# Turning depthwise kernels over on TensorE, wider Toeplitz loads, a deeper queue of rows, and an earlier place for the merging

## The chip, the core and the metric

The kernel runs on one core of one Trainium2 chip. The metric is the device time of one execution in microseconds (us), and the time before is the median of three runs. One more execution was taken by the hardware profiler; all rows below come from that one.

## The reference

The input `x` is float32, 8 images of 384 channels and 32 by 32 pixels. Four layers follow one another; everything is float32.

- Layer 0 is a two-directional state-space scan (16 states a channel over 1024 pixels) between dense projections, with a gated depthwise 3x3 convolution beside it.
- Layer 1 is a convolution block, a linear attention and a dense MLP with GELU.
- Layer 2 sums seven depthwise convolutions with their batch norms: one of 13x13 and six smaller, some dilated. All of them fit into 13x13, so the kernel merges them into one 13x13 kernel for each channel.
- Layer 3 is a 1x1 convolution with batch norm and a residual, then a depthwise 13x13 convolution with batch norm, to which a per-channel scale is added, and GELU:

```python
x_pw = bn(einsum('bchw,oc->bohw', x, pw_w), ...) + x
out = bn(dwconv(x_pw, dwk_w), ...)
out = out + bn(x_pw * dw1_w, ...)
return gelu(out, approximate=False)
```

## The kernel before, in words

**The layers 0 and 1** (`_layers01`). For each image b the function `front(b)` makes the inputs of the scan, `scan(b)` scans, and `layer1(b)` (called `seconds[b]`) does the rest. `scan(b)` has 48 units of work (`rounds = 48`), each with two steps. A step makes `da` on ScalarE (line 840), `du` on VectorE (line 845), two scans on VectorE (line 857), and one product on GpSimd (line 866); TensorE then sums over the states (lines 546, 551). Between the units a hand-written planner calls the generators in `jobs`, each given as [generator, total cost, first unit, last unit, done]: whichever is furthest behind its due share is advanced, until none is behind. During scan b, `front(b+1)` and `seconds[b-1]` are advanced. During the first scan there is also `fold()`, which folds norms into weights and fills `x2_d` with zeros. A scheduler of the framework then orders each engine's instructions; they run in that order.

**Merging the depthwise kernels** (`kernels`, called `prepare`). For each of three groups of 128 channels and for each of the two 13x13 convolutions, GpSimd clears a tile `g` (line 199 or 215), VectorE adds the scaled kernels into it with channels on partitions (`merge`, lines 184 and 186), and a DMA on GpSimd's queue writes `g` to DRAM (line 210 into `g2_d`, line 224 into `g3_d`). In DRAM the layout is [channel, 4 shifts, 63 rows, 4 taps]. The planner is told to do this with cost 7 during the second scan (units 48 to 96).

**The depthwise convolutions** (`conv`). A convolution in the direction of rows is a product with a Toeplitz matrix: for one channel, one shift e and one tap t, the 32 by 32 matrix is read out of the 63 rows by letting row j begin one row later than row j-1. `load_windows` reads such overlapping windows for a block of 8 channels: four DMAs, one for each shift, each of 32 partitions times 8 channels times 128 floats. The tile `tp` is [128, 8 channels, 32 rows x 4 taps], and there are 20 of them. The first 20 blocks are loaded by `windows` from GpSimd's queue behind the last scan, the others from the queues of SyncE and ScalarE up to ten blocks ahead (line 245).

The pixels of a block come as `xt` [128, 8, 313]: one DMA on GpSimd's queue (line 296) fills 32 partitions with the padded rows, and two VectorE copies (`shift`, line 302) make the three shifted images on the other 96. There are four such tiles and `conv` loads two blocks ahead. A block has 64 products of a 128x32 weight with 256 columns (line 326), in two PSUM tiles. The weight is

```python
tp[:, c, :].rearrange("p (j t) -> p j t", t=KT)[:, :, t]
```

so its 32 columns lie 4 floats apart.

The first convolution (tag "a", 48 blocks) evicts to `yt` on VectorE and ScalarE by turns and writes `y2_d` with one DMA for two blocks (line 344). Then the 1x1 convolution runs, 16 steps from `y2_d` to `xp_d` (lines 365 to 388). The second convolution (tag "b") reads `xp_d`; ScalarE applies GELU from PSUM into `ot` (line 394, six tiles), and GpSimd's queue writes the result, one DMA for four channels (line 395). On GpSimd's queue each `xt_b` load therefore stands between the outputs of earlier blocks, in program order.

Of the kernel before, what the change touches and what calls it, by code (L numbers as in the profile page):

```python
# [10 lines left out]
FP = mybir.dt.float32  # L11
# [29 lines left out]
N_WIN, NCH = 20, 8  # L41
N_REP, N_DA, N_HS = 6, 4, 8
AHEAD = 5000
TP = H * KT
PADW = KS // 2
HIMG = H // 2 * (W + 2)
UL = L + 6
# [21 lines left out]
def tile_layers(  # L69
# [40 lines left out]
    x2_d = dram.tile([C, H, RL], FP, tag="x2_d", name="x2_d")  # L110
    y2_d = dram.tile([C, H, B, W], FP, tag="y2_d", name="y2_d")
    xp_d = dram.tile([C, H, RL], FP, tag="xp_d", name="xp_d")
    g2_d = dram.tile([C, NSH, TG, KT], FP, tag="g2_d", name="g2_d")
    g3_d = dram.tile([C, NSH, TG, KT], FP, tag="g3_d", name="g3_d")
# [47 lines left out]

    bias2 = const.tile([P, NC, 1], FP, tag="bias2", name="bias2")

    def kernels(small, large):

        off = H - 1 - KS // 2

        def merge(g, src, k, d, scale, first):
            lo = KS // 2 - d * (k // 2)

            step = NSH // gcd(NSH, d)
            for a in range(min(step, k)):
                n = len(range(a, k, step))
                kx = lo + d * a
                dst = g[
                    :, kx % NSH, off + lo : off + lo + d * (k - 1) + 1 : d,
                    kx // NSH : kx // NSH + (n - 1) * (d * step // NSH) + 1 : d * step // NSH,  # L180
                ].rearrange("p b a -> p a b")
                sv = src[:, a::step, :]
                if first:
                    nc.vector.tensor_scalar_mul(dst, sv, scale)
                else:
                    nc.vector.scalar_tensor_tensor(dst, sv, scale, dst, ALU.mult, ALU.add)

        def column(t, n, name):
            return t[:, :n].rearrange("p (q i t) -> p q i t", q=NSH, i=TG)

        bias3 = const.tile([P, NC, 1], FP, tag="bias3", name="bias3")
        dlt = const.tile([P, NC, 1], FP, tag="dlt", name="dlt")
        gn = NSH * TG * KT
        for c in range(NC):
            kw = small(f"kw_{c}")
            ktot = sum(k * k for k, _ in _L2K)
            nc.sync.dma_start(kw[:, :ktot], l2k[c * P : (c + 1) * P, :])
            t = large(f"g2_{c}")
            nc.gpsimd.memset(t[:, :gn], 0.0)
            g = column(t, gn, "g2")  # L200
            at = 0
            for j, (k, d) in enumerate(_L2K):
                src = kw[:, at : at + k * k].rearrange("p (a b) -> p a b", b=k)
                at += k * k
                merge(g, src, k, d, bns(f"l2_{j}", c), j == 0)
# [18 lines left out]
            nc.gpsimd.dma_start(g3_d[c * P : (c + 1) * P].rearrange("p q i t -> p (q i t)"), t[:, :gn])  # L224
            yield 1
# [8 lines left out]
    def load_windows(g_d, tag, n, queues):  # L234

        if not wins:
            wins["pool"] = ctx.enter_context(tc.tile_pool(name="win", bufs=1, side="right"))
        tp = wins["pool"].tile([P, NCH, TP], FP, tag="tp", name=f"tp_{tag}_{n}", bufs=N_WIN)
        for e in range(NSH):
            at = H * ((n % 2 * 2 + e) % NSH)  # L240
            win = bass.AP(
                g_d.tensor, g_d[NCH * n, e, 0, 0].offset,
                [[KT, H], [NSH * TG * KT, NCH], [1, TP]],
            )
            queues[e % len(queues)].dma_start(tp[at : at + H], win)
        wins[tag, n] = tp

    def windows(queues):
# [8 lines left out]

    NQ = C // 4
    GB = 4
    with tc.tile_pool(name="cw", bufs=1, reuse_waits="tile") as cwp, tc.tile_pool(  # L260
        name="cx", bufs=2, reuse_waits="tile"
    ) as cxp, tc.tile_pool(
        name="cps", bufs=6, space=PSUM, reuse_waits="tile"
    ) as cps:
        xos = []
        for i in range(3):
            t = cwp.tile([P, NC, 2, RL], FP, tag=f"xo{i}", name=f"xo{i}")
# [4 lines left out]
        gbias = cwp.tile([P, NQ], FP, tag="gbias", name="gbias")  # L272
        for q in range(4):
            nc.scalar.dma_start(gbias[q * H : (q + 1) * H, :], biasq_d[q, :].partition_broadcast(H))
        def conv(g_d, src_d, tag, put):

# [8 lines left out]
            def load(n):  # L285
                for m in range(n, min(n + 1 + N_WIN // 2, NB_C)):
                    if (tag, m) not in wins:
                        load_windows(g_d, tag, m, [nc.sync, nc.scalar])
                if n >= NB_C:
                    return  # L290
                at = places(n)
                xt = cxp.tile([P, NCH, RL], FP, tag="xt", name=f"xt_{tag}_{n}", bufs=4)
                src = bass.AP(
                    src_d.tensor, src_d[NCH * n, 0, 0].offset, [[RL, H], [H * RL, NCH], [1, RL]],
                )
                nc.gpsimd.dma_start(xt[at[0] : at[0] + H], src)  # L296
                xts[n] = xt
# [7 lines left out]
                    )  # L305


            for n in range(2):
                load(n)
            shift(0)  # L310
            for g in range(NQ):
                n, first = divmod(4 * g, NCH)
                if first == 0:
                    load(n + 2)
                    if n + 1 < NB_C:
                        shift(n + 1)
                    xt, tp = xts.pop(n), wins[tag, n]
                ps = cps.tile([P, HALF], FP, tag="cv", name=f"cv_{tag}_{g}")
                for t in range(KT):
                    for e in range(4):  # L320
# [5 lines left out]
                        nc.tensor.matmul(  # L326
                            ps[H * e : H * (e + 1), 0:BW],
                            tp[:, c, :].rearrange("p (j t) -> p j t", t=KT)[:, :, t], rhs,
                            start=(t == 0), stop=(t == KT - 1), skip_group_check=True,
                        )  # L330
                put(g, ps[:, 0:BW])
# [3 lines left out]

        def put2(g, ps):
            if g % GB == 0:
                hold["t"] = cxp.tile([P, GB, BW], FP, tag="yt", name=f"yt_{g}")
            if g % 2:
                nc.scalar.copy(hold["t"][:, g % GB, :], ps)  # L340
            else:
# [21 lines left out]
        xf = xp_d.rearrange("(k p) h r -> p k h r", p=P)  # L363
        NB = 2 * BW
        for t in range(H // 2):
            yt = cxp.tile([P, NC, NB], FP, tag="yp", name=f"yp_{t}", bufs=3)
            nc.sync.dma_start(yt, yf[:, :, t * NB : (t + 1) * NB])
            xo = xos[t % 3]
            for m in range(NC):
                ps = cps.tile([P, HALF], FP, tag="cv", name=f"pw_{t}_{m}")  # L370
                for k in range(NC):
# [4 lines left out]
                tm = cxp.tile([P, NB], FP, tag="tm", name=f"tm_{t}_{m}", bufs=3)  # L376
# [19 lines left out]
                ov[g * P : (g + 1) * P], ot.rearrange("p (b w) -> p b w", w=W)  # L396
            )

        conv(g3_d, xp_d, "b", put3)


def _layers01(tc, nc, B, xv, x2_d, dram, ident, mean_w, eps5, eps6, one, half, minus1, vec, bns, bnt,
# [12 lines left out]
    with ExitStack() as ctx:  # L415
# [78 lines left out]
        def psum(name):  # L494
            return psp.tile([P, HALF], FP, tag="mm", name=name, bufs=2)
# [430 lines left out]
                nc.gpsimd.dma_start(dst.rearrange("(k p) o -> p k o", p=P), w)  # L926
                yield 5

        prepare = kernels(t2, lambda name: sp.tile([P, NC * C], FP, tag="w", name=name, bufs=N_W))

        def phi(dst, ps, name):

# [380 lines left out]
```

## Time and profile before

| what | us |
|---|---|
| median of three runs (5093.32 to 5104.8) | 5100.76 |
| the profiled execution, and its span | 5049.81, 5048.0 |
| first scan, from its first product on GpSimd to that of the second scan | 530.2 |
| second scan | 500.4 |
| third and fourth scan | 493.9 and 492.9 |
| last scan, with no `front` beside it | 426.0 |
| the rest of the last image's layer 1 | 366.6 |
| first depthwise convolution | 211.8 |
| 1x1 convolution, to the first product of the next | 150.1 |
| second depthwise convolution, to the end | 252.9 |

The stages follow one another, and the rows come from the view of windows with the starts of the first instructions as bounds. Busy shares over the whole span (PE 83%, DVE 75%, POOL 59%, ACT 52%) are averages over stages with different limits, so each stage is read by itself. In what follows PE is TensorE, PEld its weight loads, DVE is VectorE, ACT ScalarE, POOL GpSimd and SP SyncE.

### The profile page before, as it was taken

What the parts mean: (1) busy time and instruction counts of PE and PEld (TensorE: products, weight loads), DVE (VectorE), ACT (ScalarE), POOL (GpSimd) and SP (SyncE); (2) the same over time, 40 slices, a digit from 0 to 9 for tenths busy, and PEclk for the clock granted to TensorE, in tenths of its full rate; (3) what the DMA queues carried; (4) which work ended last, traced back from release to release, by engine and by line L of the source; (5) the groups of instructions that cost most, each with busy time, mean ns of one, the idle gap of its engine ahead of it and who ended that gap; (6) DMA issues with size and microseconds to landing.
All of it is one profiled execution on the core that took longest, in us unless ns stands there. A gap on an engine that the chain in (4) does not pass through costs nothing. (4 is left out here: it accounts for less than half of the span.)

```text
span 5048.0 us, 58439 instructions
## 1 busy us (share of the span) xinstructions
PE 4205.7 (83%) x20128; PEld 1787.7 (35%) x20128; DVE 3789.3 (75%) x3861; ACT 2632.2 (52%) x3735; POOL 2975.1 (59%) x1546
## 2 busy tenths in 40 slices
PE   7555568898989998988888898988888869978877
PEld 2211113332333333333333333333333324466366
DVE  1689889988988898788978887888898821066256
ACT  3546435784577557756765676568546613100211
POOL 1467567676666676666666666666776750032156
PEclk9676779899989998999899999999898979999989
DMA  8975556577657765776567646765754581399686
GB/s 229 276 235 180 178 157 208 204 219 195 216 181 217 202 215 176 215 207 217 180 199 214 223 170 195 231 211 174 181 169 133 160 177 41 71 215 233 212 189 142
DMA packets 543121, 965.28 MB, mean 191 GB/s; under 512 B 56569, under 2 KB 220905, under 8 KB 542825
## 3 DMA queue, kind: packets, MB, share of 16 engines
q1 hardware_dynamic: 401648, 663.89, 44.2%
q0 software_dynamic: 58048, 205.76, 15.4%
q10 hardware_dynamic: 83128, 91.90, 6.4%
q8 instruction: 159, 2.61, 0.2%
q14 instruction: 138, 1.12, 0.1%
HBM read 726.36 MB, written 234.98 MB: 190 GB/s over the span
## 5 line engine op out<-in xcount | busy, mean ns | idle before, releaser
L866 POOL TENSOR_TENSOR hs<-hs,bct 128x1024 f32<-128x1024 f32 x768 | 2418.2, 3149 | 939.6 <-DVE carry L862 422.9
L840 ACT ACTIVATE da<-dlt,neg_a 128x512 f32<-128x512 f32 x1536 | 1036.7, 715 | 1055.1 <-DVE hs L857 987.9
L857 DVE TENSOR_TENSOR_SCAN hs<-da,carry,du 128x512 f32<-128x512 f32 x768 | 942.7, 1266 | 175.3 <-PE acc L551 129.8
L845 DVE TENSOR_TENSOR du<-vr,bct 128x1024 f32<-128x1024 f32 x768 | 1019.2, 1327 | 46.3 <-DMA vr<-v_d 34.9
L857 DVE TENSOR_TENSOR_SCAN hs<-da,du 128x512 f32<-128x512 f32 x768 | 900.8, 1208 | 128.6 <-PE acc L551 59.9
L551 PE MATMUL acc<-hs,selt 128*32 128x512 f32 x2304 | 546.7, 663 | 140.9 <-POOL hs L866 140.7
L533 PE MATMUL mf<-ln,w 128*128 128x512 f32 x1152 | 546.1, 620 | 22.8 <-DMA w<-w_d 11.7
L1166 PE MATMUL mo<-hm,w 128*128 128x512 f32 x1152 | 530.3, 599 | 13.8 <-DVE xx L1133 13.8
L546 PE MATMUL acc<-hs,selt 128*32 128x512 f32 x768 | 428.5, 653 | 74.4 <-POOL hs L866 63.7
L533 PEld LDWEIGHTS mf<-ln,w 128*128 128x128 f32 x1152 | 222.0, 200 | 331.7 <-issue 270.4
L533 PE MATMUL in<-xn,win 128*128 128x512 f32 x576 | 295.7, 654 | 44.0 <-DMA win<-in_inproj_t 23.6
L1166 PEld LDWEIGHTS mo<-hm,w 128*128 128x128 f32 x1152 | 214.7, 190 | 307.5 <-issue 281.2
L840 ACT ACT_TABLE_LOAD x233 | 298.9, 1283 | 9.5 <-DMA dw_i<-h_d 3.0
L326 PE MATMUL cv_b<-xt_b,tp_b 128*32 128x256 f32 x3072 | 193.6, 407 | 67.9 <-DVE xt_b L302 44.1
L302 DVE COPY xt_b<-xt_b 32x2496 f32<-32x2496 f32 x96 | 147.8, 1540 | 108.0 <-DMA xt_b<-xp_d 103.9
L326 PE MATMUL cv_a<-xt_a,tp_a 128*32 128x256 f32 x3072 | 186.0, 390 | 47.6 <-DVE xt_a L302 21.4
L1136 POOL DMA_DIRECT2D x_d<-xx x48 | 56.5, 1179 | 281.4 <-DVE xx L1133 274.1
L551 PE MATMUL dw<-dw_i,t3b 96*32 96x512 f32 x1056 | 205.6, 656 | 11.1 <-DMA dw_i<-h_d 11.0
L533 PE MATMUL op<-g,wo 128*128 128x512 f32 x288 | 156.4, 695 | 61.3 <-DMA g<-g_d 61.3
L326 PEld LDWEIGHTS cv_b<-xt_b,tp_b 128*32 128x32 f32 x3072 | 163.8, 141 | 98.0 <-issue 69.3
L533 PEld LDWEIGHTS in<-xn,win 128*128 128x128 f32 x576 | 114.1, 207 | 215.2 <-issue 161.5
L326 PEld LDWEIGHTS cv_a<-xt_a,tp_a 128*32 128x32 f32 x3072 | 159.7, 138 | 74.3 <-issue 28.7
(196 smaller groups left out, 5724.7 us busy)
## 6 DMA issues: line engine op xcount, KB each, us to landing
dlt<-dl_d SPq DMA_DIRECT2D x384, 256.0 KB, 4.6
vr<-v_d SPq DMA_DIRECT2D x384, 256.0 KB, 5.0
bct<-bc_d SPq DMA_DIRECT2D x256, 256.0 KB, 3.7
ut<-u_d SPq DMA_DIRECT2D x192, 257.5 KB, 5.5
lc_i<-xn_d SPq DMA_DIRECT2D x192, 228.8 KB, 5.4
dw_i<-h_d SPq DMA_DIRECT2D x192, 228.8 KB, 5.6
w<-w_d SPq DMA_DIRECT2D x64, 576.0 KB, 6.1
w<-in_w SPq DMA_DIRECT2D x64, 576.0 KB, 5.9
```

The source lines that it names most:

```text
L302: nc.vector.tensor_copy(xt[at[e] : at[e] + e * H, :, 0 : RL - e - (e - 1)], xt[at[0] : at[0] + e * H, :, e : RL - (e - 1)],)
L326: nc.tensor.matmul(ps[H * e : H * (e + 1), 0:BW], tp[:, c, :].rearrange("p (j t) -> p j t", t=KT)[:, :, t], rhs, start=(t == 0), stop=(t = ...
L533: product = nc.tensor.matmul(ps, w[:, k, m * P : (m + 1) * P], rhs[k] if isinstance(rhs, list) else rhs[:, k, :], start=(k == 0), stop=(k ...
L546: first = product()
L551: tc.keep_in_program_order(product())
L840: nc.scalar.activation(da[:, bass.ts(j, HALF)], dlt[:, bass.ts(j, HALF)], AF.Exp, scale=neg_a[:, g, r : r + 1],)
L845: nc.vector.tensor_mul(pairs(du), pairs(vt), bct[r][:, 0:1, :].to_broadcast([P, 2, HALF]),)
L857: nc.vector.tensor_tensor_scan(t[:, s][:, way], da[:, s][:, way], du[:, s][:, way], k_c if second else 0.0, ALU.mult, ALU.add,)
L866: made.append(nc.gpsimd.tensor_mul(pairs(t), pairs(t), bct[r][:, 1:2, :].to_broadcast([P, 2, HALF])))
L1136: nc.gpsimd.dma_start(x2v[m, :, h * (H // 2) : (h + 1) * (H // 2), PADW + b * (W + PADW) : PADW + b * (W + PADW) + W,], rows(o),)
L1166: nc.tensor.matmul(acc[m], wb[:, f, m * P : (m + 1) * P], hm, start=(i == 0 and f == 0), stop=(i == FF // C - 1 and f == NC - 1),)
```

## The change

- `kernels` gets a PSUM allocator. After a kernel tile `g` is merged, `put_columns` turns it over: for each of the four shifts, four products with the identity put [63 rows, 128 channels] for each tap into PSUM, VectorE copies them into a tile in the order channel, tap, and a DMA on GpSimd's queue writes that tile to DRAM. `g2_d` and `g3_d` become [48 blocks, 4 shifts, 63 rows, 8 channels x 4 taps].
- `load_windows` reads, for each of the 32 partitions, one contiguous piece of 32 rows x 8 channels x 4 taps (4096 bytes); `tp` becomes [128, 32 rows, 8 channels, 4 taps], and the weight is `tp[:, :, c, t]`, whose columns lie 32 floats apart.
- `conv` takes the distance of its loads as `far`: 2 for the first convolution and 5 for the second. The second has three more tiles for rows, `xu`, in the place of the pool `cw`, which is closed after the 1x1 convolution; the tiles `yt`, `yp` and `tm` move into that pool.
- The planner is told to merge with cost 31 during the first scan (units 0 to 48).

```diff
-    g2_d = dram.tile([C, NSH, TG, KT], FP, tag="g2_d", name="g2_d")
+    g2_d = dram.tile([C // NCH, NSH, TG, NCH * KT], FP, tag="g2_d", name="g2_d")
...
+        def put_columns(g_d, g, c, name):
+            for q in range(NSH):
+                ps = psum(f"{name}_{c}_{q}")
+                for t in range(KT):
+                    nc.tensor.matmul(
+                        ps[:TG, t * P : (t + 1) * P], g[:, q, :, t], ident, start=True, stop=True,
+                        skip_group_check=True,
+                    )
+                o = small(f"{name}t_{c}_{q}")
+                nc.vector.tensor_copy(
+                    o[:TG, :].rearrange("i (c t) -> i t c", t=KT), ps[:TG, :].rearrange("i (t c) -> i t c", t=KT)
+                )
+                nb = P // NCH
+                nc.gpsimd.dma_start(
+                    g_d[c * nb : (c + 1) * nb, q].rearrange("n i e -> i n e"),
+                    o[:TG, :].rearrange("i (n e) -> i n e", n=nb),
+                )
...
-            nc.gpsimd.dma_start(g2_d[c * P : (c + 1) * P].rearrange("p q i t -> p (q i t)"), t[:, :gn])
-            yield 1
+            put_columns(g2_d, g, c, "p2")
+            yield 5
...
-        tp = wins["pool"].tile([P, NCH, TP], FP, tag="tp", name=f"tp_{tag}_{n}", bufs=N_WIN)
+        tp = wins["pool"].tile([P, H, NCH, KT], FP, tag="tp", name=f"tp_{tag}_{n}", bufs=N_WIN)
...
             win = bass.AP(
-                g_d.tensor, g_d[NCH * n, e, 0, 0].offset,
-                [[KT, H], [NSH * TG * KT, NCH], [1, TP]],
+                g_d.tensor, g_d[n, e, 0, 0].offset, [[NCH * KT, H], [1, H * NCH * KT]],
             )
...
-                xt = cxp.tile([P, NCH, RL], FP, tag="xt", name=f"xt_{tag}_{n}", bufs=4)
+                if "pool" in more and n % 7 >= 4:
+                    xt = more["pool"].tile([P, NCH, RL], FP, tag="xu", name=f"xt_{tag}_{n}")
+                else:
+                    xt = cxp.tile([P, NCH, RL], FP, tag="xt", name=f"xt_{tag}_{n}", bufs=4)
...
-                    load(n + 2)
+                    load(n + far)
...
-                            tp[:, c, :].rearrange("p (j t) -> p j t", t=KT)[:, :, t], rhs,
+                            tp[:, :, c, t], rhs,
...
-        conv(g2_d, x2_d, "a", put2)
+        conv(g2_d, x2_d, "a", put2, 2)
...
-        conv(g3_d, xp_d, "b", put3)
+        mid_ctx.close()
+        with tc.tile_pool(name="xu", bufs=3, reuse_waits="tile") as more["pool"]:
+            conv(g3_d, xp_d, "b", put3, 5)
...
-        jobs = [[fold(), 36, 0, rounds, 0], [prepare, 7, rounds, 2 * rounds, 0]]
+        jobs = [[fold(), 36, 0, rounds, 0], [prepare, 31, 0, rounds, 0]]
```

More of the change, by code (lines that the diff above doesn't have):

```diff
@@ L43 @@
 AHEAD = 5000
-TP = H * KT
 PADW = KS // 2
@@ L112, in tile_layers @@
     xp_d = dram.tile([C, H, RL], FP, tag="xp_d", name="xp_d")
-    g2_d = dram.tile([C, NSH, TG, KT], FP, tag="g2_d", name="g2_d")
-    g3_d = dram.tile([C, NSH, TG, KT], FP, tag="g3_d", name="g3_d")
+    g2_d = dram.tile([C // NCH, NSH, TG, NCH * KT], FP, tag="g2_d", name="g2_d")
+    g3_d = dram.tile([C // NCH, NSH, TG, NCH * KT], FP, tag="g3_d", name="g3_d")
     bias_d = dram.tile([C], FP, tag="bias_d", name="bias_d")
@@ L163, in tile_layers, with kernels @@
     bias2 = const.tile([P, NC, 1], FP, tag="bias2", name="bias2")
-    def kernels(small, large):
+    def kernels(small, large, psum):
         off = H - 1 - KS // 2
@@ L223, in kernels @@
             nc.vector.tensor_add(bias3[:, c, :], bnt("dwk", c), bnt("dw1", c))
-            nc.gpsimd.dma_start(g3_d[c * P : (c + 1) * P].rearrange("p q i t -> p (q i t)"), t[:, :gn])
-            yield 1
+            put_columns(g3_d, g, c, "p3")
+            yield 5
         with nc.allow_non_contiguous_dma(reason="384 biases"):
@@ L241, in load_windows @@
             win = bass.AP(
-                g_d.tensor, g_d[NCH * n, e, 0, 0].offset,
-                [[KT, H], [NSH * TG * KT, NCH], [1, TP]],
-            )
-            queues[e % len(queues)].dma_start(tp[at : at + H], win)
+                g_d.tensor, g_d[n, e, 0, 0].offset, [[NCH * KT, H], [1, H * NCH * KT]],
+            )
+            queues[e % len(queues)].dma_start(
+                tp[at : at + H].rearrange("p j c t -> p (j c t)"), win
+            )
         wins[tag, n] = tp
@@ L259, in tile_layers @@
     GB = 4
-    with tc.tile_pool(name="cw", bufs=1, reuse_waits="tile") as cwp, tc.tile_pool(
-        name="cx", bufs=2, reuse_waits="tile"
-    ) as cxp, tc.tile_pool(
+    with tc.tile_pool(name="cx", bufs=2, reuse_waits="tile") as cxp, tc.tile_pool(
         name="cps", bufs=6, space=PSUM, reuse_waits="tile"
     ) as cps:
+        gbias = cxp.tile([P, NQ], FP, tag="gbias", name="gbias", bufs=1)
+        mid_ctx = ExitStack()
+        cwp = mid_ctx.enter_context(tc.tile_pool(name="cw", bufs=1, reuse_waits="tile"))
+        more = {}
         xos = []
@@ L271, in tile_layers, with conv @@
         nc.scalar.dma_start(pwt, pw_t.rearrange("(k p) o -> p k o", p=P))
-        gbias = cwp.tile([P, NQ], FP, tag="gbias", name="gbias")
         for q in range(4):
             nc.scalar.dma_start(gbias[q * H : (q + 1) * H, :], biasq_d[q, :].partition_broadcast(H))
-        def conv(g_d, src_d, tag, put):
+        def conv(g_d, src_d, tag, put, far):
             xts = {}
@@ L305, in shift @@
                     )
-            for n in range(2):
+            for n in range(far):
                 load(n)
@@ L337, in put2 @@
             if g % GB == 0:
-                hold["t"] = cxp.tile([P, GB, BW], FP, tag="yt", name=f"yt_{g}")
+                hold["t"] = cwp.tile([P, GB, BW], FP, tag="yt", name=f"yt_{g}", bufs=2)
             if g % 2:
@@ L365, in tile_layers @@
         for t in range(H // 2):
-            yt = cxp.tile([P, NC, NB], FP, tag="yp", name=f"yp_{t}", bufs=3)
+            yt = cwp.tile([P, NC, NB], FP, tag="yp", name=f"yp_{t}", bufs=3)
             nc.sync.dma_start(yt, yf[:, :, t * NB : (t + 1) * NB])
@@ L375, in tile_layers @@
                     )
-                tm = cxp.tile([P, NB], FP, tag="tm", name=f"tm_{t}_{m}", bufs=3)
+                tm = cwp.tile([P, NB], FP, tag="tm", name=f"tm_{t}_{m}", bufs=3)
                 nc.scalar.activation(
@@ L927, in fold @@
                 yield 5
-        prepare = kernels(t2, lambda name: sp.tile([P, NC * C], FP, tag="w", name=name, bufs=N_W))
+        prepare = kernels(t2, lambda name: sp.tile([P, NC * C], FP, tag="w", name=name, bufs=N_W), psum)
         def phi(dst, ps, name):
```

## The prediction

> **What bounds the kernel now.** I read the busy shares by stage first (view of windows: length, busy us of PE, PEld, DVE, ACT, POOL, granted clock, DMA share, GB/s). The rows below are scan one, two and three, the first depthwise convolution ("a") and the second ("b").
>
> ```profile
> 145.60:675.80 530.20, 296.50 (x1048) 92.74 (x1048) 458.31 (x433) 263.80 (x372) 330.87 (x164) 0.68 0.63 202
> 675.80:1176.20 500.40, 434.14 (x1668) 164.88 (x1669) 435.81 (x480) 320.66 (x444) 341.18 (x160) 0.92 0.67 202
> 1176.20:1670.10 493.90, 442.21 (x1698) 169.66 (x1697) 425.03 (x423) 323.59 (x448) 332.68 (x148) 0.94 0.67 203
> ...
> 4433.20:4645.00 211.80, 185.52 (x3070) 159.70 (x3072) 155.69 (x142) 17.51 (x47) 65.89 (x68) 0.98 1.08 244
> ...
> 4795.10:5048.00 252.90, 193.55 (x3072) 163.74 (x3072) 144.85 (x94) 45.49 (x96) 154.84 (x140) 0.94 0.79 165
> ```
>
> Both convolutions do the same 3072 products, but b takes 41 us more; in b no engine and no DMA is full. In scan one PE is light (297 of 530) and DVE is the fullest (458). Next the page's costliest groups, for who is waited for in b:
>
> ```profile
> L326 PE MATMUL cv_b<-xt_b,tp_b 128*32 128x256 f32 x3072 | 193.6, 407 | 67.9 <-DVE xt_b L302 44.1
> L302 DVE COPY xt_b<-xt_b 32x2496 f32<-32x2496 f32 x96 | 147.8, 1540 | 108.0 <-DMA xt_b<-xp_d 103.9
> ```
>
> PE waits for the shift, and the shift for the landing of the rows. The timelines of PE, DVE and POOL show why:
>
> ```profile
> 4846.75 4.93 PE L326 MATMUL cv_b<-xt_b,tp_b 128*32 128x256 f32 x82
> 4856.28 6.02 PE L326 MATMUL cv_b<-xt_b,tp_b 128*32 128x256 f32 x74 [4.61 <-DVE xt_b L302]
> ```
>
> ```profile
> 4852.91 3.27 DVE L302 COPY xt_b<-xt_b 32x2496 f32<-32x2496 f32 x2 [5.99 <-DMA xt_b<-xp_d]
> ```
>
> ```profile
> 4847.39 0.59 POOL L296 DMA_DIRECT2D xt_b<-xp_d  x1
> 4847.98 1.86 POOL L395 DMA_DIRECT2D out<-ot  x2
> 4849.83 0.59 POOL L296 DMA_DIRECT2D xt_b<-xp_d  x1
> 4850.75 0.89 POOL L395 DMA_DIRECT2D out<-ot  x1 [0.33 <-ACT ot L394]
> 4852.56 0.89 POOL L395 DMA_DIRECT2D out<-ot  x1 [0.92 <-ACT ot L394]
> 4853.43 1.42 POOL L296 DMA_DIRECT2D xt_b<-xp_d  x1
> 4860.42 0.92 POOL L395 DMA_DIRECT2D out<-ot  x1 [5.57 <-ACT ot L394]
> ```
>
> It is a ring. A load is issued only after outputs that wait for ACT, which waits for PE; the load issued at 4847.39 landed at 4852.8, its two copies ended at 4856.2, and PE, which had run dry 4.6 us before, began. With loads two blocks ahead the ring (issue, 5.6 us median to landing, two copies of 1.45) is longer than two blocks of PE work. After the stop PE also runs at half pace for about 4 us: four products start every 0.43 us there, every 0.215 us elsewhere. Blocks come in threes of about 8.5, 5.2 and 3.5 us, and the shortest, 3.48, is PE's own pace (16 x 0.2155).
>
> **Second convolution, far = 5.** The ring is cut: seven tiles, loads five blocks ahead, at least 17 us for a chain of about 9. What is late next? For a block: PE 3.48. DVE two copies, 2.9. POOL one load and two outputs. Alone these cost 0.593 and 0.888, 2.37 in all; but of the 48 loads the 27 that overlap a DVE copy have a mean of 1.32, and of the 96 outputs the 59 that do have 1.30. DVE will copy for some 75% of the time, so I take the overlapped row: 1.32 + 2 x 1.30 = 3.9 us, and POOL becomes the bound by a little. DMA: the stage moved 165 GB/s x 252.9 us = 41.7 MB; in 193 us that is 216 GB/s, and a moves 244 with smaller pieces. So 48 x 3.9 plus the 5.7 from the last product to the end = 193, **-60**. Bounds: PE's pace 3.48 gives 173 (-80); a's present pace, 211.8/48 = 4.41, gives 217 (-35).
>
> The Trainium skill (SBUF — State Buffer, sections "SBUF: two separate sides" and "A bandwidth-pool intuition that's wrong") speaks against this: a DMA issued from GpSimd's queue cannot write its descriptors while a float32 SBUF copy on VectorE holds their shared port, and it gives some 3.1 us for such an issue instead of 0.62. By that figure three issues would cost 9.3 us a block, and the stage would be 452 us by my estimate from it. The row for it here is the 1.30 to 1.32 us above, at most 2.16; the measured rows decide.
>
> **Windows in one piece.** In the first convolution 48,225 of the 58,268 DMA packets are 512 bytes, 44 ns each, 61% of the engines' time; the packets of 4096 bytes there take 47 ns a KB against 88. DMA is at 1.08, so landings (8.0 us for `xt_a`) should get shorter. But a is not bound there: the order of DVE's queue is the same in the changed program, and in it a shift stands behind an eviction that waits for PE. The repeating four blocks take 17.5 us, of which one wait for a landing is 0.68. Twelve times 0.68 is 8; I take **-4**, bounds -12 and 0. The 80 window DMAs on POOL behind the last scan (0.58 each) have nobody waiting behind them; 0, or -5 if the 15.5 us for which PE waits on `g_d` there shrink.
>
> The weights' columns now lie 128 bytes apart instead of 16. The trace has no such load. Contiguous 128x32 loads take 114 ns (`acc`), those 16 bytes apart 138 and 141. From below the cost is 0; from above I take the same step once more, 28 ns. Products start every 54 ns with four loads overlapping, so 28 ns would be 6144 x 28 / 4 = 43 us. I take 0: the step already separates all columns, and it is nearest to the row of 16 bytes.
> The Trainium skill (SBUF — State Buffer, section "Door 1: The DMA port swizzle", on 16-byte lines) says that each access crossing into a new line of 16 bytes pays a penalty; by it both layouts pay alike, and the cost is 0. No run here shows that.
>
> **Scans one and two.** The merging has 75 DVE operations, 36.9 us (12 forms summed in the groups of 600 to 1060 us). But the scheduler already begins them at 618: only 7.75 + 6.38 = 14.1 us lie in the second scan, and 22.8 at the end of the first. So the first scan gets 14 us of DVE more, and 24 new copies from PSUM: the nearest row, `zr<-acc` 128x512 out of PSUM, is 0.68, so 16.5 us (10 at the 256-column row, 33 if the reordering doubles it). DVE has 530.2 - 458.3 = 72 us idle there, mostly in the first 120 us, where the fill of `x2_d` has DMA at 0.8 to 0.98; the first of the six groups falls there. I put half of the 31 on the path: +15.
> POOL issues 24 DMAs instead of 6: nearest rows are 1.18 (`x_d<-xx`, 128x16x32 pieces) and 0.76 (`xn_d<-zero`), so 18 to 28 us, less 6 x 0.55. They stand between the products of line 866 and wait for the DVE copy, which waits for PE: while such a DMA waits, the next scan products wait on POOL, then PE's sums. POOL is 331 of 530 busy and can catch up; I take one us for each group of four, +6.
> PE gets 96 products 63x128; at the 0.28 us of a 128x128 weight load these are 27 us in a stage with 230 idle: 0. Without that cover, 27.
> The second scan loses its merging and should be like its followers: 500.4 to 493.4, -7.
> Sum for the scans **+14**, from -7 (all in idle time) to about +50.
>
> **Total.** -60 - 4 + 14 = -50. The profiled execution, 5049.8, would be 5000. The three runs had a median of 5100.8, 1.0% above it; by the same microseconds that gives 5050. A change of less than 0.2%, 10 us, can't be told from none (the three runs themselves spread over 11.5).
>
> **Rivals.**
> - *The first scan pays for everything.* The ring DVE to POOL to PE there is tight, and every hand-over of `put_columns` (two PSUM tiles, shared with `front`) stalls it: 31 of DVE, 25 of POOL and 24 hand-overs of 2 us, 104 - 7 = +97. Total +33: 5134. It decides from the point where the first scan is longer than 530 + 64 + 7 = 601 us. For it: DVE 86% busy, merges of up to 2.3 us where a POOL product was running. Against: the 14 us in scan two cost only 7. Chance 0.14.
> - *Only the wait changes its name in b.* POOL stays in order, with outputs that wait for ACT, so that the pace is that of the last sixteen blocks now, 4.68: 48 x 4.68 + 5.7 = 230, -22. Total -12: 5089. Against it: those blocks still waited for landings. Chance 0.14.
> - *The weight loads slow PE*, both convolutions by 43 us (-7 in total, 5094), or by 172 if nothing overlaps (5223). From 50 us / 6144 = 8 ns a product it is no gain. Chance 0.06.
> - *All of it hidden*, b at 3.48: -80 - 8 - 7 = -95, 5006. Chance 0.10.
> - The forecast, 5050, its own range 5015 to 5085: 0.56.
>
> **Range and chances.** 5008 to 5100 leaves out the first rival, most of the third, and half of the last. Faster: 0.55 of the forecast, 0.08 of the second rival, 0.01 and 0.10, 0.74. Slower: 0.14 + 0.04 + 0.01 = 0.19. The rest, 0.07, is no difference.
>
> **What would show it.** Right: b near 193 us with few waits of the shifts on `xp_d`, POOL over 85% busy in it, issue times of 1.3; a at 205 to 211 with packets of 4 KB; scan one 545 to 560, scan two about 493; PEld of `cv_a` still near 138 ns. Wrong: b still over 225, scan one over 600, or products of b starting more than 60 ns apart inside a block.

## The result and the profile after

The changed kernel takes 5057.56 us (median of four runs, 5055.1 to 5066.84), beside 5102.78 us for the kernel before in the same session (5093.32 to 5114.69). The ratio is 0.9914, with a 95% interval of 0.9889 to 0.9938: it is faster, by 45 us. Run a second time, as e4 below, it gave 0.9900 [0.9884, 0.9917], 51 us. The forecast was 5050, 50 us faster.

The profiled execution took 5066.84 us, its span 5065.1. The profile of the kernel before came from an execution 1% shorter than the median of its runs (5049.81 against 5100.76), so differences of stages are taken from a second profile of the kernel before, e0 (span 5143.5, scans three to six 503 to 506 us as in the changed kernel, where they are 502 to 509). Stages by the bounds of the table of before, in us; only a and the 1x1 convolution part at the first product of the 1x1 here, some 11 us later than there:

| stage | before, e0 | after | after again, e4 | e4 - e0 |
|---|---|---|---|---|
| first scan | 532.4 | 562.4 | 566.3 | +34 |
| second scan | 506.2 | 490.2 | 492.0 | -14 |
| scans three to eight | 2945.7 | 2934.7 | 2948.9 | +3 |
| rest of the last image's layer 1 | 377.8 | 360.0 | 362.7 | -15 |
| a, from its first product to the first of the 1x1 | 229.7 | 222.5 | 222.3 | -7 |
| 1x1 convolution | 140.5 | 139.1 | 139.9 | -1 |
| b, to the end | 258.0 | 203.9 | 205.0 | -53 |
| start | 153.1 | 152.4 | 151.3 | -2 |

The last column adds up to -55, the difference of the two spans (5143.5 - 5088.5); the medians give 51. e0 and e4 come from two sessions (medians of before 5129.92 and 5140.79), and the profiled execution of e0 was the slowest of its eight (5145.33, median 5133.21), so a difference of a few us may be the spread of the profiles. Against the first profile of before, the rest of layer 1 (366.6 there, 360.0 after) gains 7 us, and a (222.8 to the first product of the 1x1, 222.5 after) nothing. It is the forecast's picture, with other sizes: b gives the gain, the first scan gives some back, and a stage to which the forecast gave nothing gives up to 15 us more.

The view of windows of the changed kernel, with the columns as before (length, busy us of PE, PEld, DVE, ACT, POOL, granted clock of PE as a share of full speed, mean busy share of the DMA engines, GB/s). The rows are scan one, two and three, a to its last product, and b:

```profile
152.40:714.80 562.40, 329.21 (x1267) 122.96 (x1264) 488.97 (x517) 267.59 (x375) 360.81 (x191) 0.71 0.67 201
714.80:1205.00 490.20, 427.52 (x1641) 159.44 (x1640) 425.84 (x420) 313.74 (x439) 331.65 (x148) 0.93 0.64 196
1205.00:1709.20 504.20, 446.14 (x1698) 168.85 (x1697) 425.25 (x423) 322.80 (x447) 332.52 (x150) 0.94 0.68 199
4499.50:4711.50 212.00, 185.49 (x3072) 158.44 (x3072) 155.88 (x142) 17.50 (x47) 62.10 (x68) 0.98 0.93 244
4861.20:5065.10 203.90, 180.84 (x3072) 156.30 (x3072) 147.15 (x94) 45.16 (x96) 190.18 (x138) 0.98 0.85 205
```

The last row is to be read against the 252.9 of before. There no engine was full; here POOL is busy 190 of 204 us, 93%. It issues the same loads and outputs as before (154.84 us then), so they have grown longer. The DMA engines moved 244 GB/s in a as it did before, with a share of 0.93 in place of 1.08: the larger pieces are cheaper for the DMA engines.

The costliest groups answer to the two lines of before in the prediction; the second one's wait for landings has fallen from 103.9 to 49.8 us, and PE's wait for the shift from 44.1 to 16.9 (13.8 of it, both times, ahead of b's first product):

```profile
L351 PE MATMUL cv_b<-xt_b,tp_b 128*32 128x256 f32 x3072 | 180.8, 388 | 29.0 <-DVE xt_b L327 16.9
L327 DVE COPY xt_b<-xt_b 32x2496 f32<-32x2496 f32 x96 | 150.1, 1564 | 54.1 <-DMA xt_b<-xp_d 49.8
...
L351 PEld LDWEIGHTS cv_b<-xt_b,tp_b 128*32 128x32 f32 x3072 | 156.3, 137 | 53.9 <-issue 31.6
```

The third line is the weight load with columns 128 bytes apart: 137 ns, where it was 141.

The timelines of POOL, DVE and PE in the middle of b (start, length, instruction; in brackets the idle time ahead of it) show what takes the place of the ring:

```profile
4952.40 1.76 POOL L420 DMA_DIRECT2D out<-ot  x2
4954.15 0.59 POOL L321 DMA_DIRECT2D xt_b<-xp_d  x1
4954.74 3.81 POOL L420 DMA_DIRECT2D out<-ot  x2
4958.54 0.59 POOL L321 DMA_DIRECT2D xt_b<-xp_d  x1
4959.13 3.83 POOL L420 DMA_DIRECT2D out<-ot  x2
4962.94 0.59 POOL L321 DMA_DIRECT2D xt_b<-xp_d  x1
```

```profile
4954.89 3.18 DVE L327 COPY xt_b<-xt_b 32x2496 f32<-32x2496 f32 x2 [3.54 <-DMA xt_b<-xp_d]
4959.29 3.19 DVE L327 COPY xt_b<-xt_b 32x2496 f32<-32x2496 f32 x2 [1.22 <-DMA xt_b<-xp_d]
```

```profile
4958.28 3.84 PE L351 MATMUL cv_b<-xt_b,tp_b 128*32 128x256 f32 x64 [2.64 <-issue]
4962.68 3.85 PE L351 MATMUL cv_b<-xt_b,tp_b 128*32 128x256 f32 x64 [0.56 <-PE cv_b L351]
```

POOL has no gap, and nothing in brackets. Two outputs take 1.76 us with no copy on DVE, and 3.81 while the two copies run beside them. The second output ends 0.48 us after the second copy, both times (4958.55 against 4958.07, 4962.96 against 4962.48). A block is one load and two outputs, here 4.40 us, and PE, which needs 3.48 us for a block, gets one in that time. The ring is gone; POOL's queue is what is late next.

### The profile page after: what moved, and what is told of

Its sections match the earlier page's. It is cut to its first block, busy times and chain, and to the rows that moved or that the text cites. A ratio compares the mean times of both kernels' runs of the same rounds, so it can differ in the third digit from the quotient of the medians.

```text
span 5065.1 us, 58926 instructions
## 1 busy us (share of the span) xinstructions
PE 4238.9 (84%) x20320; PEld 1806.8 (36%) x20320; DVE 3814.7 (75%) x3885; ACT 2628.7 (52%) x3732; POOL 3020.6 (60%) x1564
## 3 DMA queue, kind: packets, MB, share of 16 engines
q14 instruction: 137, 1.12, 0.1%
## 5 line engine op out<-in xcount | busy, mean ns | idle before, releaser
L872 DVE TENSOR_TENSOR du<-vr,bct 128x1024 f32<-128x1024 f32 x768 | 1032.1, 1344 | 35.7 <-DMA vr<-v_d 19.2
L560 PEld LDWEIGHTS mf<-ln,w 128*128 128x128 f32 x1152 | 222.8, 200 | 337.1 <-issue 270.1
L578 PE MATMUL dw<-dw_i,t3b 96*32 96x512 f32 x1056 | 201.8, 626 | 10.7 <-DMA dw_i<-h_d 10.3
L351 PE MATMUL cv_b<-xt_b,tp_b 128*32 128x256 f32 x3072 | 180.8, 388 | 29.0 <-DVE xt_b L327 16.9
L327 DVE COPY xt_b<-xt_b 32x2496 f32<-32x2496 f32 x96 | 150.1, 1564 | 54.1 <-DMA xt_b<-xp_d 49.8
```

Of the source, the lines that this page charges most:

```text
L327: nc.vector.tensor_copy(xt[at[e] : at[e] + e * H, :, 0 : RL - e - (e - 1)], xt[at[0] : at[0] + e * H, :, e : RL - (e - 1)],)
L351: nc.tensor.matmul(ps[H * e : H * (e + 1), 0:BW], tp[:, :, c, t], rhs, start=(t == 0), stop=(t == KT - 1), skip_group_check=True,)
L560: product = nc.tensor.matmul(ps, w[:, k, m * P : (m + 1) * P], rhs[k] if isinstance(rhs, list) else rhs[:, k, :], start=(k == 0), stop=(k ...
L578: tc.keep_in_program_order(product())
L872: nc.vector.tensor_mul(pairs(du), pairs(vt), bct[r][:, 0:1, :].to_broadcast([P, 2, HALF]),)
```

## The experiments

Each was compared with the kernel before in the same session, so ratios can be set beside one another, and times of different sessions cannot; "rows" are the tiles of pixels.

**e0, the kernel before once more.** No edit.

> The kernel before once more, for a profile on the same chip as the others. The profile of the changed kernel has scans three to six 7 to 12 us longer each (502 to 508 against 493 to 498), though the change touches nothing in them. Theory: the two profiles were taken under other conditions; here these scans take 500 to 508, too, and the span is 5085 to 5110. Rival: the change itself slows the later scans (other places in memory); then they stay at 493 to 498 here.

Measured: 1.0001 [0.9985, 1.0018]. Scans three to six take 503 to 506 us, as the theory had it; the span, 5143.5, is longer than it expected. This profile is the control of the table above.

**e1, only the deeper queue of rows in b.** Before, with

```diff
-                    load(n + 2)
+                    load(n + far)
...
-        conv(g3_d, xp_d, "b", put3)
+        mid_ctx.close()
+        with tc.tile_pool(name="xu", bufs=3, reuse_waits="tile") as more["pool"]:
+            conv(g3_d, xp_d, "b", put3, 5)
```

> The kernel before with the deeper queue of rows alone (far = 5 and three more tiles in the second convolution; old layout, old merging). Theory: the whole gain comes from here; the second convolution falls from 253 to 200 to 210 us and the time by 40 to 55 us. Rival: with windows in pieces of 512 bytes the DMA engines are full at that pace, so that the deeper queue needs the new layout; then the second convolution stays above 225 and the gain is 25 or less.

Measured: 5100.68, ratio 0.9939 [0.9918, 0.9959]. The window of b in its profile:

```profile
4893.30:5110.50 217.20, 184.43 (x3072) 154.39 (x3072) 146.52 (x94) 45.08 (x96) 170.14 (x138) 0.96 0.92 193
```

258.0 becomes 217.2: in b the deeper queue by itself is worth 41 us, which lies between the theory (200 to 210) and the rival (over 225). The time falls by 29 us in the medians (5129.92 to 5100.68), less than the theory's 40 to 55; in the profile the span is 33 us shorter, since other stages are some 8 us longer than in e0. Of the 53 us that the whole change gains in b, 12 come only with the new layout. In e1's b, waits of ACT that end with the landing of a window (`ACT ot <- DMA tp_b<-g_d`) add up to 80.0 us, in the changed kernel's to 3.1; that points to the landings of the windows, but no run separates them.

**e2, only the layout, made in the second scan.** After, with `far` 2 in b, no `xu`, and the merging in the second scan:

```diff
-                if "pool" in more and n % 7 >= 4:
+                if "pool" in more and n < 0:
...
-            conv(g3_d, xp_d, "b", put3, 5)
+            conv(g3_d, xp_d, "b", put3, 2)
...
-        jobs = [[fold(), 36, 0, rounds, 0], [prepare, 31, 0, rounds, 0]]
+        jobs = [[fold(), 36, 0, rounds, 0], [prepare, 31, rounds, 2 * rounds, 0]]
```

> The new layout alone (kernels turned over on TensorE, windows in one piece), merged in the second scan as before, loads two blocks ahead in both convolutions. Theory: the layout buys nothing: first convolution 210 to 213, second 245 to 255, and the second scan pays 10 to 20 us for the copies and the 24 DMAs; the time rises by 5 to 20 us. Rival: shorter landings shorten the ring of the second convolution; 235 or less there, and the time falls by 5 to 15 us.

Measured: 5169.82, ratio 1.0076 [1.0054, 1.0098]: slower by 40 us, where the theory had 5 to 20. Its second scan is 557.0 (e0 506.2); its b is 250.3, its a 223.0, its rest of layer 1 367.9. So the layout brings 7 us in a, 8 in b and 10 ahead of a, where the theory had it buy nothing, and turning the kernels over costs some 50 in that scan, where it had 10 to 20.

**e3, all of the change but the early place.** After, with the `jobs` line of e2.

> The changed kernel with its merging put back into the second scan (cost 31, units 48 to 96). Theory: the first scan is the worse place, since VectorE and GpSimd are its bound; first scan back to about 530, second 505 to 515, and the time 5 to 20 us below that of the changed kernel. Rival: the second scan, with a full TensorE, pays more; the time is 5 to 15 us above the changed kernel.

Measured: 5125.4, ratio 0.9985 [0.9972, 0.9999]. I had held the first scan, where DVE is 86% busy, for the worse place, and it is the better one by 36 us in the profiles and by more in the ratios (0.9985 here, 0.9900 in e4): here scans one and two take 534.8 + 560.2 = 1095.0 us, in e4 566.3 + 492.0 = 1058.3. The window of e3's second scan, and under it that of e0:

```profile
684.10:1244.30 560.20, 469.93 (x1864) 194.81 (x1865) 470.56 (x505) 327.65 (x451) 358.24 (x177) 0.91 0.64 182
```

```profile
685.50:1191.70 506.20, 436.69 (x1668) 164.53 (x1669) 436.31 (x480) 320.15 (x444) 341.04 (x159) 0.91 0.67 199
```

PE is 84% busy there (470 of 560) where it is 59% in the first scan, and DVE is no less full: the second scan has both.

**e4, the changed kernel once more.** No edit.

> The changed kernel once more, on one chip with the next three. Theory: ratio to the kernel before between 0.989 and 0.994; scans one and two together 10 to 20 us longer than in the kernel before, the second convolution about 50 us shorter, the first and the rest of layer 1 together 15 to 25 us shorter, other scans alike. Rival: the first measurement caught a better placement by luck; the ratio is above 0.995 here.

Measured: 5090.28, ratio 0.9900 [0.9884, 0.9917]. The stages are as the theory had them (last column of the table).

**e5, only the early place, old layout.** Before, with

```diff
-        jobs = [[fold(), 36, 0, rounds, 0], [prepare, 7, rounds, 2 * rounds, 0]]
+        jobs = [[fold(), 36, 0, rounds, 0], [prepare, 7, 0, rounds, 0]]
```

> The kernel before with one thing moved: the old merging (cost 7, old layout, no turning over) in the first scan instead of the second. Theory: without TensorE's products and the copies the place hardly matters; scans one and two together within 8 us of the kernel before, the time within 10 us. Rival: the early place is a gain by itself, since the second scan has a full TensorE and a VectorE at 86%: the time is 12 to 25 us lower.

Measured: 5115.03, ratio 0.9950 [0.9934, 0.9965]. One line of the planner gives 26 us, and the rival holds. Scans one and two in its profile:

```profile
150.00:679.30 529.30, 301.55 (x1070) 95.30 (x1066) 471.29 (x493) 272.93 (x379) 335.11 (x173) 0.70 0.69 213
679.30:1167.90 488.60, 425.58 (x1644) 160.70 (x1645) 424.74 (x420) 314.46 (x438) 332.15 (x149) 0.93 0.65 197
```

They are 20.7 us shorter than in e0: the first does not get longer by taking all of the merging, the second gets 17.6 shorter. Against this the scans of e4 are 40.4 longer (37.0 and 3.4). That is the price of turning the kernels over, in the better of the two places and with the planner's cost of 31 in place of 7; the other profiles with the same two scans (after, e6, e7, e10) give 35 to 44.

**e6, the outputs of b on SP's queue.** After, with

```diff
-            nc.gpsimd.dma_start(
+            nc.sync.dma_start(
                 ov[g * P : (g + 1) * P], ot.rearrange("p (b w) -> p b w", w=W)
```

> The changed kernel with the 96 outputs of the second convolution issued from SyncE's queue instead of GpSimd's. Theory: GpSimd's issues beside VectorE's copies (190 of 204 us) set the pace there; with 48 loads alone on that queue the second convolution falls to 178 to 190 us and the time by 12 to 25 us below the changed kernel. Rival: the landing of the outputs is what holds ScalarE (70 us of waits for the tiles of the output), and that is DMA time; then the stage stays at 198 us or more.

Measured: 5075.3, ratio 0.9872 [0.9859, 0.9886], the lowest ratio of all that was run. It is ahead of the changed kernel's 0.9900 by about 0.3% (15 us, as the theory had it), with intervals that barely overlap; e7 and e8 cannot be told from it. Its window of b, and the longest of the waits there (who waited for whom: us in total, times, longest):

```profile
4876.90:5071.20 194.30, 180.78 (x3072) 147.80 (x3072) 136.54 (x94) 44.22 (x96) 41.25 (x41) 0.98 1.05 215
```

```profile
POOL xt_b L321 <- PE cv_b L351: 102.3, 33, 9.0
ACT ot L419 <- PE cv_b L351: 62.5, 28, 16.7
ACT ot L419 <- DMA out<-ot: 60.2, 40, 6.4
```

POOL falls to 41 us and b from 205.0 to 194.3, which is between what the two theories expected: POOL's queue was the limit, and 10.7 us behind it the next one begins. What that is was not tested: POOL's loads now wait for PE to give tiles back, ACT still waits for outputs to land, and the DMA share is 1.05. DVE's copies get shorter too (146.9 us in e4, 136.5 here): outputs and copies had held each other up.

**e7, twelve tiles `ot` in place of six.** After, with

```diff
-            ot = cxp.tile([P, BW], FP, tag="ot", name=f"ot_{g}", bufs=6)
+            ot = cxp.tile([P, BW], FP, tag="ot", name=f"ot_{g}", bufs=12)
```

> The changed kernel with twelve output tiles instead of six in the second convolution. Theory (GpSimd's queue is the bound): more tiles only make the queue longer; ScalarE's waits for them shrink, but the stage stays at 196 to 206 us and the time within 6 us of the changed kernel. Rival (the landings are the bound): the stage falls to 180 to 190 us.

Measured: 5077.78, ratio 0.9877 [0.9863, 0.9890]; the interval overlaps that of e4. The median is 12.5 us below e4's, where the theory had at most 6; b accounts for 3 of them. In the changed kernel's b, ACT waits for outputs to land, which it did not in the kernel before. Here are the first two rows of the view of waits of after; the second fence is e7:

```profile
ACT ot L419 <- PE cv_b L351: 88.3, 34, 16.6
ACT ot L419 <- DMA out<-ot: 70.2, 45, 3.2
```

```profile
ACT ot L419 <- PE cv_b L351: 142.1, 83, 16.8
...
ACT ot L419 <- DMA out<-ot: 8.0, 6, 1.3
```

The wait of 70 us goes to 8, and b from 205.0 (203.9 in after) only to 202.1: ACT waits for PE instead. That wait was a consequence of POOL's pace and not a second limit.

**e8, the products that turn over made twice.** After, with

```diff
-                for t in range(KT):
+                for t in [i for i in range(KT) for _ in range(2)]:
```

> The changed kernel with every turning product done twice (first scan). Theory: TensorE has cover in the first scan (330 of 566 us busy), so some 38 us more of TensorE cost 0 to 10 us there; the time is within 10 us of the changed kernel (ratio to the kernel before 0.988 to 0.994). Rival: the hand-overs run through TensorE's queue; 20 us or more.

Measured: 5069.7, ratio 0.9885 [0.9864, 0.9905], the same as e4 within the intervals. Scans one and two take 545.7 + 498.9 = 1044.6 us, no more than e4's 1058.3, with 192 records of these products more. Its first scan, to be read beside that of the changed kernel above (562.40):

```profile
152.50:698.30 545.80, 335.42 (x1460) 147.48 (x1456) 483.13 (x517) 271.54 (x378) 358.90 (x192) 0.74 0.69 207
```

More of these products cost no time in the first scan. Their records grow from 36.1 to 58.2 us, and yet PE is busy only 6 us longer: its other work there took 277 us in place of 293, and the mean granted clock is 0.74 in place of 0.71. Whether PE's part is hidden in idle time or paid back by shorter other work was not separated, and why the sum is 14 us lower is open.

**e9, the same with the merging in the second scan.** e8's edit and e2's `jobs` line.

> The same with the merging in the second scan, where TensorE is 86% busy before anything is added. Theory: there the products are on the path; the second scan grows from 560 to 585 to 600 us, ratio to the kernel before 1.003 to 1.008. Rival: the cost of the second scan comes from the copies and hand-overs; it stays below 572.

Measured: 5130.72, ratio 1.0003 [0.9990, 1.0016]. The second scan takes 573.7 us, with PE busy 493.12; in e3 it is 560.2 with 469.93. So 23 us more of PE go with 13.5 more there, which lies between the two theories: by these two profiles somewhat more than half of PE's part is on the path (the same scan in e2 is 557.0, so some 3 us are spread). These products are 29.7 us busy in e3, so by that share they are some 17 of its 54 us (an estimate from the two profiles); what the copies, the DMAs and the hand-overs have of the rest was not separated.

**e10, all evictions of a on ScalarE.** After, with

```diff
-            if g % 2:
+            if True:
                 nc.scalar.copy(hold["t"][:, g % GB, :], ps)
```

> The changed kernel with all evictions of the first convolution on ScalarE. Theory: the shifts there stand behind evictions on VectorE that wait for TensorE; without them the first convolution (222 us to the first product of the 1x1) falls to 190 to 205 and the time by 15 to 30 us below the changed kernel. Rival: the DMA engines (0.93 busy, 244 GB/s) or the two blocks of distance bind it; it stays at 215 or more.

Measured: 5108.02, ratio 0.9961 [0.9946, 0.9976]. a gets longer, from 222.3 to 232.6, as the rival had it. The ratio is 0.6% above e4's, some 31 us, of which a shows 10; the rest is not explained. Two rows of the view of waits in a, e10 first and then e4:

```profile
DVE xt_a L327 <- DMA xt_a<-x_d: 79.1, 31, 8.0
...
PE cv_a L351 <- DVE xt_a L327: 44.9, 6, 24.8
```

```profile
PE cv_a L351 <- DVE xt_a L327: 24.7, 1, 24.7
...
DVE xt_a L327 <- DMA xt_a<-x_d: 7.2, 5, 3.3
```

In both, one wait of PE of almost 25 us lies ahead of a's first product; within a, PE waits 20 us for shifts in e10 and not at all in e4. With no eviction ahead of them the shifts wait for landings instead, 79 us in place of 7. So the evictions on DVE were not what held a.

**e11, the old layout with everything else.** Before, with the early place of e5, the deeper queue of e1, the outputs of e6 and the evictions of e10.

> The kernel before with its old layout, the early merging, the deeper queue of rows, the outputs of the second convolution on SyncE's queue and all evictions of the first on ScalarE: everything that helped, without the turning over. Theory: the turning over and the layout cost about as much in the scans (40 us) as they bring behind them (12 + 7 + 15), so this is at or below the changed kernel with the same two additions; scans one and two together about 1018, second convolution 200 to 212, ratio to the kernel before 0.980 to 0.987. Rival: with pieces of 512 bytes the DMA engines bind both convolutions once the waits are gone (first at 225 or more, second at 215 or more); ratio 0.987 to 0.991.

Measured: 5078.48, ratio 0.9902 [0.9885, 0.9918]. Beside e6: scans one and two 526.8 + 489.0 = 1015.8 against 1062.0, the rest of layer 1 373.5 against 362.8, a 236.6 against 219.6, b 211.3 against 194.3. The ratio is the rival's and not the theory's, with a above the 225 of the rival and b below its 215. The evictions of e10 cost something here too: 10 us by e10's a, 31 by its ratio. Without them the old layout would be at a ratio of 0.988 or 0.984 by my estimate from these two numbers, level with e6's 0.9872 or below it; that kernel was not run, so which layout is the better one stays open.

## Why the prediction was right, and where its sizes were wrong

That the total came within 5 us of the measured 45 and 51 is in part luck: b gave less than forecast, the scans cost up to 6 us more, and a stage that the sum had at nothing made up for it.

**The second convolution (-60 forecast, -53 measured).** The ring and what comes behind it were read rightly: waits of the shifts halved, POOL over 90% busy, ACT not the limit. Within POOL's work two sizes were off and nearly cancel. For outputs beside copies I took the mean of before, 1.30 us; in the changed kernel the 75 of the 96 outputs that overlap a DVE copy have a mean of 1.67, at most 2.17, and the 21 others 0.89. So the outputs took 75 x 1.665 + 21 x 0.888 = 143.5 us, where the sum had 96 x 1.30 = 125. The 48 loads have 1.07 (the overlapped ones 1.31, as forecast), and 6 of them are issued ahead of the stage; the other 42 took 47.8, where the sum had 48 x 1.32 = 63. POOL is busy 190.2 us, where the sum had 187. What the forecast lacked is POOL's idle time: 13.7 us of the stage (203.9 - 190.2), of which 4.5 lie at the start, before the first eviction, 5.1 behind the last issue, and some 4 between, where the sum had 5.7 in all.

The trace also shows why 1.30 was no price for one issue. Of the 75 outputs that overlap a copy, 65 are lengthened, and each of these ends 0.48 us after the end of a copy; each lengthened load ends 0.15 us after one (26 of 26). So a lengthened issue is held until the copy has ended. The others overlap a copy that ends in their first 0.46 us or begins 0.24 us or more after their start, and take 0.89, as if alone. The mean of before mixed 33 lengthened outputs (1.62 on average) with 26 such others; when DVE copies most of the time, 65 of 96 are lengthened, to 1.78 on average.

The Trainium skill (SBUF — State Buffer, sections "SBUF: two separate sides" and "A bandwidth-pool intuition that's wrong") has such an issue blocked until the copy on VectorE ends; the 0.48 and 0.15 us above agree with it. Its 3.1 us is not seen here, where the longest output takes 2.17 us, beside copies of some 1.5.

**The first convolution (-4 forecast, -7 measured).** The size lies in its bounds, by luck: the reason did not hold, and against the first profile of before a gains nothing. I said that a is bound by the order of DVE's queue, a shift standing behind an eviction that waits for PE. e10 takes that order away and a is 10 us longer. A chain of issue, landing and two copies with loads two blocks ahead, as it was in b (landings 7.5 us in the median in e4, 8.9 in e0), would fit both results, but no run gave a the deeper queue: what binds a stays open.

**The rest of layer 1 (0 forecast, -15 measured; -7 against the first profile of before).** This term was mis-sized most. I looked for someone waiting behind the window DMAs on POOL, found nobody, and gave them no price, or 5 us if PE's wait on `g_d` shrank; it shrank by 3, from 17.8 in e0 to 14.9 in e4. Groups in that stage, e0 first and e4 below:

```profile
L245 POOL DMA_DIRECT2D tp_a<-g_d x80 | 46.5, 583 | 28.4 <-DMA tp_a<-g_d 18.6 <-issue 5.0 <-PE acc L551 1.8
L551 PE MATMUL dw<-dw_i,t3b 96*32 96x512 f32 x132 | 34.9, 814 | 5.6 <-DMA dw_i<-h_d 5.6
```

```profile
L264 POOL DMA_DIRECT2D tp_a<-g_d x80 | 39.1, 491 | 25.7 <-DMA tp_a<-g_d 16.8 <-issue 3.8 <-PE acc L578 2.7
...
L578 PE MATMUL dw<-dw_i,t3b 96*32 96x512 f32 x132 | 26.7, 667 | 5.0 <-DMA dw_i<-h_d 5.0
```

The issues get 0.09 us shorter, which is 7 us of POOL; and the products of layer 1's own depthwise convolution, whose inputs come by DMA in the same stretch, take 667 ns in place of 814. The mean granted clock of the stage is 0.90 in e4 and 0.87 in e0. Through what the 15 us came was not tested; the products alone do not explain them, for in after they take 784 ns and the stage is no longer than in e4 (360.0). That the layout brings the gain is shown by the experiments: the stage takes 360.0 to 367.9 in the nine profiles with it, and 373.5 to 381.6 in four without (e0, e1, e5, e11). The fifth without it, the first profile of before, has 366.6, but its scans three to eight are 2% shorter than in e0, too.

**The weights 128 bytes apart (0 forecast, 0 measured).** 137 ns against 139 and 142 in e0. The Trainium skill (SBUF — State Buffer, section "Door 1: The DMA port swizzle") says that each access crossing to a new line of 16 bytes pays a penalty; that both layouts pay alike, as I concluded from it, agrees with these rows. The third rival is out.

**Scans one and two (+14 forecast, +14 to +20 measured).** The sum is right by errors that cancel. I had +21 for the first scan and -7 for the second; measured were +34 and -14 in e4, +30 and -16 in after. Two terms failed. The early place is a gain by itself (e5, -20.7): I put half of the merging's 14 us of DVE on the first scan's path and 7 us to the credit of the second; the first scan does not get longer by it, and the second gives back 17.6. Turning over costs some 40, not the 14 that are left of my sum (half of 16.5, and 6): the copies are 1.07 us, not 0.68, and the DMAs 1.12 (within 0.76 to 1.18) with waits for the copies on POOL. The groups of the changed kernel's first scan:

```profile
L206 POOL DMA_DIRECT2D g_d<-p2t x12 | 13.4, 1119 | 23.1 <-DVE p2t L202 14.2 <-DVE du L872 7.5 <-DVE carry L889 1.4
L202 DVE COPY p3t<-p 63x512 f32<-63x512 f32 x12 | 12.8, 1082 | 4.4 <-PE p L197 4.4
L202 DVE COPY p2t<-p 63x512 f32<-63x512 f32 x12 | 12.4, 1067 | 0.6 <-PE p L197 0.5
```

25 us of copies, 27 of DMAs and 28 of POOL's idle time ahead of these DMAs (23.1 and the 4.9 of the other group) lie among the steps of the scan, and the time grew by 40. PE's 27 forecast are 36 by their records (two for each product), and making them twice cost no time (e8). What each of the others has of the 40 was not separated. The first rival had +97 here with the same mechanism, a tight ring of hand-overs, and the point from which it decides, 601 us, was not reached.

**The other rivals.** "The wait only changes its name" would have made b 230; POOL's outputs wait for ACT only 8.3 us in the changed kernel's b (104.6 in e0). "All hidden" would have made b 173; even with the outputs off POOL's queue (e6) it is 194.

## What to carry to other kernels

When a ring of queue order is cut, look next at the busiest queue in it. Price its issues beside what will then run against them all the time, not by their mean in a stage that stalls, and count the idle time at the start and the end of the stage. A layout that makes loads cheaper has a price where it is made: here turning the kernels over cost some 40 us in the scans and brought about 34 (12 in b, 7 in a, 15 ahead of a), so nearly all of the net gain came from the deeper queue (41 in b, 29 in the medians) and the planner's early place (21 in the profile, 26 in the medians). Ask of each part of a change whether it pays by itself, and put background work where the fewest engines are full together: scans one and two were 36 us shorter with it in the first, with PE at 59%, than in the second, with PE at 84%.

## What the runs showed of the hardware that was not expected

- A DMA issued from GpSimd's queue for an output of 128x256 takes 0.89 us alone and a mean of 1.67 (at most 2.17) while VectorE copies within SBUF. Every lengthened one of the changed kernel ends 0.48 us after the end of a copy (65 of 65), every lengthened load 0.15 us after one (26 of 26).
- With the outputs issued from SyncE's queue instead, VectorE's copies in that stage take 1.45 us, where the two of a block take 1.53 and 1.60 in e4. The longest, 1.9 us (before and e4), begin 0.24 us into the issue of an output.
- A VectorE copy out of PSUM that reorders 63x512 values takes 1.07 us. An operation on 128x512 that reads PSUM in plain order and a second input (`zr<-acc,zr`) takes 0.68, and a plain copy of 128x256 (`yt<-cv_a`) 0.42.
- With pieces of 4096 bytes in place of 512 the DMA share in a falls from 1.08 to 0.93 at the same 244 GB/s, and a hardly gains; what gains is a stage before it, in which the same loads fly beside dense work.
